# A spectral layer's results on four 64x64 TensorE tiles, and a last stage with small end chunks and zero-padded matmuls

## The chip, the cores and the metric

The kernel runs on one core of one Trainium2 chip. The metric is the time of one execution on the device, in microseconds (us). Before the change it is 1813.42 us, the median of three runs (1812.36 to 1813.81). The profiled execution took 1810.9 us; its trace spans 1809.2 us from the first to the last instruction, and every position in time below is counted from that span's start.

## What is computed

The input is an image batch of 4 x 56 x 56 positions with 128 channels, fp32. Layer 0 normalises in groups and adds a 7 x 7 neighbourhood attention. Layer 1 sees the image as 3136 tokens; it adds a linear attention, and then a spectral filter whose result is added to the same tokens:

```python
t = t + _L1_attn_ref(_ln_t(t), ...)
t = t + _L1_ffn_ref(_ln_t(t), ...)   # causal convolutions by FFT, 16 filters, then 128x128 matrices
```

Only the spectral filter's last part and the final sum are touched here. The convolution is done as small Fourier transforms, written as matmuls against constant tables. The image's rows and columns are transformed separately: 42 row frequencies (`N1 = 42`), and for each of them 28 column points (`NM = 28`), with real and imaginary parts, for two halves of the rows (`NS = 2`), two column parities `p`, four images and 128 channels.

## The kernel before

The program has three stages. `layers` (to about 780 us) does both attentions and the forward row transforms. `spectral_layer` (about 780 to 1658 us) goes over the 42 row frequencies. `onto_the_rest` (about 1659 us to the end) transforms back over the rows and adds the result to the tokens.

**The spectral loop** (L1570) is a software pipeline with one pass of the loop for one row frequency, 20.33 us each. TensorE's order is the program's own there (`manual_schedule` for PE); the other engines' orders are chosen when the program is built. A pass does, on TensorE: eight times `matrices` (L1487) alternating with seven times `product` (L1510); then `token_points` (L1466) for the next frequency; then `columns` (L1536) for the frequency three passes back. `columns` transforms results back over the columns: four matmuls, one for each row half `s` and column parity `p`, with 56 rows and 56 columns of the array in use and 512 moving columns. Operands of parity `p` lie in partitions 64p to 64p+55, and so do the results, so parity 0 uses the array's upper left quarter and parity 1 its lower right one. Each result has a PSUM bank of its own, and four copies (`evacuate`, L167 to L174, alternately on ScalarE and VectorE) bring them to `zs`. `store_columns` (L1554) writes `zs` to `zd` in DRAM.

PSUM has eight banks: three called `g0`, three `g1`, one `x`, one `py`. Each `g` name is handed out in turn, so a request gets the bank of the third request before it. `matrices` takes two `g0` and two `g1` at each call. `token_points` takes `x` and one `g0` and fills both; VectorE copies them to `us` (L1481), and ScalarE makes a negated copy of a part (L1482, `nc.scalar.mul`). `columns` takes two `g1` and two `g0`. So the first `g0` of the next pass's first `matrices` call is the bank that `token_points` had, and the second is that of the first parity-1 result of `columns`.

**The last stage** (L1600) loads 28 pairs of image columns in seven chunks of four (`WC = 4`). For each chunk and each half `q` of the width it loads tokens `tl` (ScalarE's DMA queue) and spectra `z` (SyncE's queue; 84 partitions, 1344 KB), does for each pair of columns four matmuls (84 rows, 56 columns, 512 moving columns; halves `q` in PSUM partitions 0 and 64), multiplies and adds on VectorE (L1634), and stores the chunk (L1639). The pool has three buffers for each name. It takes its memory after the spectral pools are given back, and as a whole.

Of the kernel before, what the change touches and what calls it, by code (L numbers as in the profile page):

```python
# [10 lines left out]
F32 = mybir.dt.float32  # L11
# [4 lines left out]
P = 128  # L16
B, H, W, C = 4, 56, 56, 128
# [39 lines left out]
NS, BR = 2, H // 2  # L57
N1, N2, NM = 42, W, W // 2
# [6 lines left out]
HALF = 2 * NM  # L65


def spectral_tables():

    m1 = np.arange(N1)  # L70
    m = m1[:, None] + N1 * np.arange(NM)[None]
    row = np.exp(-2j * np.pi * (m1[None] + 0.25) * np.arange(H)[:, None] / N1)
    rows = np.stack([row.real, row.imag], 1)
    into = np.zeros((P, 2 * N1))
    for g in range(NG):
        into[32 * g : 32 * g + BR] = rows[:BR].reshape(BR, -1)
    tok, back = np.zeros((2, N1, P, 2, NM))
    fil = np.zeros((N1, P, 2, NM, 2))
    for p in range(2):
        col = np.arange(p, N2, 2)  # L80

        fwd = np.exp(-2j * np.pi * (m[:, None, :] + 0.25) * col[None, :, None] / (2 * NP))

        bwd = np.exp(2j * np.pi * (m[:, :, None] + 0.25) * col[None, None, :] / (2 * NP)) / NP
        for part, turn in enumerate((1, 1j)):
            at = slice(64 * p + NM * part, 64 * p + NM * (part + 1))
            for to, a in ((tok, turn * fwd), (back, turn * bwd)):
                to[:, at] = np.stack([a.real, a.imag], 2)

            a = turn * fwd  # L90
            fil[:, 64 * part + NM * p : 64 * part + NM * (p + 1), p] = np.stack([a.real, a.imag], 3)

    onto = np.zeros((2, N1, NS, H))
    for s in range(NS):
        at = np.arange(H - BR * s)
        e = np.exp(2j * np.pi * (m1[:, None] + 0.25) * at[None] / N1)
        onto[0, :, s, BR * s :] = e.real
        onto[1, :, s, BR * s :] = -e.imag
    sign = np.ones((P, 1))
    sign[BR:N2] = sign[64 + BR : 64 + N2] = -1.0  # L100
    f = lambda a: np.ascontiguousarray(a, np.float32)
    return {
        "into": f(into),
        "taps_in": f(rows.reshape(H, -1)),
        "tok": f(tok.reshape(N1, P, -1).transpose(1, 0, 2)),
        "fil": f(fil.reshape(N1, P, -1).transpose(1, 0, 2)),
        "back": f(back.reshape(N1, P, -1).transpose(1, 0, 2)),
        "onto": f(onto.reshape(2 * N1, -1)),
        "sign": f(sign),
    }  # L110
# [13 lines left out]
def hybrid_kernel(  # L124
# [23 lines left out]
    nc = tc.nc  # L148
# [19 lines left out]
    def evacuate(dst, src):  # L168

        flip[0] ^= 1  # L170
        if flip[0]:
            nc.scalar.copy(dst, src)  # L172
        else:
            nc.vector.tensor_copy(dst, src)  # L174
# [1238 lines left out]
    def spectral_layer():  # L1413


        with ExitStack() as ph:
# [37 lines left out]
            def parts():  # L1454

                for p in range(2):
                    for part in range(2):
                        yield slice(64 * p + NM * part, 64 * p + NM * (part + 1)), p, part
# [77 lines left out]
            def columns(m1, yg, zs, pz):  # L1536

                back = tables_of(m1)[2]
                for s in range(NS):
                    for p in range(2):  # L1540
                        at = slice(64 * p, 64 * p + HALF)
                        nc.tensor.matmul(  # L1542
                            pz[s][p][at],
                            back[at],
                            yg[at, s * B : (s + 1) * B].rearrange("p k e -> p (k e)"),
                            start=True,
                            stop=True,
                        )
                for s in range(NS):
                    for p in range(2):  # L1550
                        at = slice(64 * p, 64 * p + HALF)
                        evacuate(zs[at, s], pz[s][p][at])

            def store_columns(m1, zs):  # L1554
                for at, p, part in parts():
                    nc.sync.dma_start(
                        zd[p::2, part * N1 + m1].rearrange("w s b e -> w (s b e)"),
                        zs[at].rearrange("w s f -> w (s f)"),
                    )

            def bank(tag):
                if tag == "x":
# [6 lines left out]
            with tc.manual_schedule(engines={mybir.EngineType.PE}):  # L1569
                for it in range(-1, N1 + LAG):  # L1570
                    ap, az, au = it - 1, it - LAG, it + 1
                    if 0 <= it < N1:
                        gts[it] = sp.tile([P, 2, 2 * NM, C // 2, 2], F32, name="gt")
                        if it + 2 < N1:
                            xms[it + 2] = load_tokens(it + 2)
                    if 0 <= ap < N1:
                        ys = sp.tile([P, NM // 4, C], F32, name="ys")
                    if 0 <= az < N1:
                        zs = sp.tile([P, NS, B * C], F32, name="zs")
                    for n in range(8):  # L1580
                        if 0 <= it < N1:
                            matrices(it, gts[it], n)
                        if 0 <= ap < N1 and n < 7:
                            if n % 4 == 0:
                                py = ps_y.tile([P, 4, C], F32, name="py")
                            product(py, gts[ap], us2[ap % 2], n)
                            if n == 3 or n == 6:
                                evacuate(ys[:, n - n % 4 : n + 1], py[:, : n % 4 + 1])
                    if au < N1:
                        token_points(au, xms.pop(au), us2[au % 2], [bank("x"), bank("g0")])  # L1590
                    if 0 <= az < N1:
                        pz = [[bank(f"g{1 - p}") for p in range(2)] for s in range(NS)]
                        columns(az, ygs.pop(az), zs, pz)
                    if 0 <= ap < N1:
                        ygs[ap] = regroup(ap, ys)
                    if 0 <= az < N1:
                        store_columns(az, zs)
                    gts.pop(ap, None)

    def onto_the_rest():  # L1600

        with ExitStack() as ph:
            fin = ph.enter_context(tc.tile_pool(name="fin", bufs=3))
            ps_o = ph.enter_context(tc.tile_pool(name="ps_o", bufs=4, space=bass.MemoryType.PSUM))
            onto = fin.tile([2 * N1, NS, H], F32, name="onto", bufs=1)
            nc.sync.dma_start(onto, table["onto"].rearrange("p (s h) -> p s h", s=NS))
            rows_in = td.rearrange("b (h w) c -> h b w c", w=W)
            rows_out = ot.rearrange("b (h w) c -> h b w c", w=W)
            WC = 4
            for w0 in range(0, W // 2, WC):  # L1610
                tl = fin.tile([P, B, WC, C], F32, name="tl")
                zin = []
                for q in range(2):
                    ws = slice(q * BR + w0, q * BR + w0 + WC)
                    nc.scalar.dma_start(tl[64 * q : 64 * q + H], rows_in[:, :, ws])
                    z = fin.tile([2 * N1, WC, NS, B * C], F32, tag=f"z{q}", name=f"z{q}")
                    nc.sync.dma_start(
                        z, zd[ws].rearrange("w p s b e -> p w s (b e)")
                    )
                    zin.append(z)  # L1620
                for i in range(WC):
                    po = ps_o.tile([P, B, C], F32, name="po2")
                    for s in range(NS):
                        for q in range(2):
                            nc.tensor.matmul(  # L1625
                                po[64 * q : 64 * q + H].rearrange("p b c -> p (b c)"),
                                onto[:, s],
                                zin[q][:, i, s],
                                start=(s == 0),
                                stop=(s == NS - 1),  # L1630
                            )
                    for q in range(2):
                        at = slice(64 * q, 64 * q + H)
                        nc.vector.scalar_tensor_tensor(  # L1634
                            tl[at, :, i], po[at], hmask[at], tl[at, :, i], ALU.mult, ALU.add
                        )
                for q in range(2):
                    ws = slice(q * BR + w0, q * BR + w0 + WC)
                    nc.scalar.dma_start(rows_out[:, :, ws], tl[64 * q : 64 * q + H])  # L1639

    unfit = keep.tile([1, 1], mybir.dt.int32, name="unfit")
    layers(False, unfit)
# [61 lines left out]
```

## Time and profile before

| Stretch | us | PE busy | clock granted to PE | DMA busy share |
|---|---|---|---|---|
| 0 to 100 | 100 | 68.08 | 0.81 | 0.55 |
| 100 to 700 | 600 | 542.73 | 0.93 | 0.45 |
| 700 to 800 | 100 | 75.22 | 0.67 | 0.53 |
| 800 to 1680 | 880 | 854.11 | 0.98 | 0.38 |
| 1680 to 1780 | 100 | 97.72 | 0.50 | 0.90 |
| 1780 to 1809.2 | 29.2 | 20.03 | 0.50 | 0.48 |

PE is the matmul engine, PEld its weight loads, DVE is VectorE, ACT is ScalarE, POOL is GpSimd, SP is SyncE. An fp32 matmul of the program shows as two records. [...]records overlap; so PE can look fully busy while it does less than it could. The granted clock is a share of TensorE's full speed. The DMA share is over the core's 16 DMA engines. A line of the trace that ends in "[0.98 <-ACT us L1482]" says that the engine was idle for 0.98 us and that the instruction of that name released it.

### The profile page before, as it was taken

How to read it: one execution, taken by the hardware profiler on the slowest of the kernel's cores; microseconds unless marked ns; L12 is line 12 of the kernel's file. 1: busy time of each engine (PE TensorE's matmuls, PEld its weight loads, DVE VectorE, ACT ScalarE, POOL GpSimd, SP SyncE). 2: the span in 40 equal slices, each digit the busy share in tenths (PEclk: the TensorE clock that was granted, in tenths of full speed). 3: DMA queues.
4: the chain of work that ended last, by engine and by line, in shares of the span. 5: the costliest groups of instructions: out<-in, count | busy, mean ns of one | idle time of the engine just before them, and what ended most of it. 6: DMA issues, size and time to landing. Idle time of an engine off the chain costs nothing. (4 is left out here: it accounts for less than half of the span.)

```text
span 1809.2 us, 71326 instructions
## 1 busy us (share of the span) xinstructions
PE 1657.9 (92%) x31481; PEld 1237.5 (68%) x31481; DVE 1070.5 (59%) x2142; ACT 756.3 (42%) x1529; POOL 390.3 (22%) x803
## 2 busy tenths in 40 slices
PE   4887898899999998779999999999999999995997
PEld 3665677567867766368888887888888887883221
DVE  4776786678868764135666666565666666562232
ACT  2333533366455444324444544454444544451000
POOL 4242254437446434000010001000000001000000
PEclk9788989899999997659999999999999999997555
DMA  6545446544343334632333333433434333325996
GB/s 166 116 88 106 86 94 147 121 119 124 88 136 91 92 98 112 198 92 65 99 106 105 96 87 100 113 99 88 102 104 107 89 91 97 103 72 150 239 226 182
DMA packets 285099, 207.69 MB, mean 115 GB/s; under 512 B 105868, under 2 KB 255532, under 8 KB 284652
## 3 DMA queue, kind: packets, MB, share of 16 engines
q1 hardware_dynamic: 275876, 189.50, 41.1%
q10 hardware_dynamic: 8904, 13.53, 2.7%
q8 instruction: 250, 4.10, 1.0%
q14 instruction: 69, 0.57, 0.1%
HBM read 115.31 MB, written 87.64 MB: 112 GB/s over the span
## 5 line engine op out<-in xcount | busy, mean ns | idle before, releaser
L1505 DVE COPY gt<-pg 128x448 f32<-128x448 f32 x672 | 388.4, 619 | 303.3 <-PE pg L1495 303.3
L1505 ACT COPY gt<-pg 128x448 f32<-128x448 f32 x672 | 326.0, 538 | 358.1 <-PE pg L1495 358.1
L1495 PE MATMUL pg<-v,mats 32*128 32x112 f32 x10752 | 402.2, 286 | 5.6 <-DVE gt L1505 2.0
L1495 PEld LDWEIGHTS pg<-v,mats 32*128 32x128 f32 x10752 | 341.8, 190 | 93.3 <-issue 51.7
L1514 PE MATMUL py<-gt,us 128*32 128x128 f32 x9408 | 339.2, 283 | 0.8 <-ACT ys L172 0.8
L1514 PEld LDWEIGHTS py<-gt,us 128*32 128x32 f32 x9408 | 266.9, 137 | 32.9 <-ACT ys L172 1.0
L1484 POOL COPY us<-us 128x448 f32<-128x448 f32 x42 | 23.4, 556 | 819.7 <-DVE us L1481 819.7
L1165 ACT ACTIVATE e<-scores 126x768 f32<-126x768 f32 (+1 forms) x140 | 107.3, 767 | 117.6 <-PE scores L1149 91.7
L1169 DVE TENSOR_TENSOR e<-e,relb 126x768 f32<-126x768 f32 (+1 forms) x140 | 137.9, 986 | 28.8 <-ACT e L1165 28.2
L1625 PE MATMUL po<-z,onto 84*56 84x512 f32 x224 | 124.8, 1067 | 20.8 <-DMA tl<-td 16.0
L1193 DVE RECIPROCAL recs<-results 128x96 f32<-128x96 f32 (+1 forms) x140 | 99.5, 711 | 49.4 <-PE results L1179 48.5
L1149 PE MATMUL scores<-qT,kp 32*126 32x96 f32 (+1 forms) x2240 | 105.0, 300 | 7.9 <-ACT e L1165 7.4
L1149 PEld LDWEIGHTS scores<-qT,kp 32*126 32x126 f32 (+1 forms) x2240 | 81.4, 196 | 43.9 <-ACT e L1165 17.9
L1625 PEld LDWEIGHTS po<-z,onto 84*56 84x56 f32 x224 | 31.8, 207 | 113.8 <-issue 98.1
L1634 DVE SCALAR_TENSOR_TENSOR tl<-po,hmask,tl 56x512 f32<-56x512 f32 x56 | 42.0, 750 | 104.4 <-PE po L1625 103.8
L1472 PE MATMUL px<-tok,xm 56*128 56x56 f32 x672 | 86.8, 281 | 18.1 <-DMA v<-vd 18.1
L1472 PEld LDWEIGHTS px<-tok,xm 56*128 56x128 f32 x672 | 81.3, 194 | 24.2 <-issue 19.9
L1179 PE MATMUL results<-e,v_sb 126*32 126x96 f32 (+1 forms) x2240 | 78.7, 261 | 11.7 <-DVE aT L1194 10.2
L1542 PE MATMUL xx<-yg,back 56*56 56x512 f32 x336 | 83.5, 611 | 4.0 <-DMA yg<-yd 4.0
L1472 PE MATMUL xx<-tok,xm 56*128 56x56 f32 x672 | 86.9, 281 | 0.0
L812 PE MATMUL bk<-mu,ut 128*112 128x128 f32 x672 | 81.8, 279 | 3.5 <-POOL ut L798 1.5
L812 PEld LDWEIGHTS bk<-mu,ut 128*112 128x112 f32 x672 | 77.0, 185 | 7.0 <-POOL ut L798 1.7
(177 smaller groups left out, 2106.1 us busy)
## 6 DMA issues: line engine op xcount, KB each, us to landing
xd<-xs SPq DMA_DIRECT2D x112, 168.0 KB
xm<-xd SPq DMA_DIRECT2D x168, 112.0 KB
yd<-ys SPq DMA_DIRECT2D x168, 112.0 KB
yg<-yd SPq DMA_DIRECT2D x168, 112.0 KB
zd<-zs SPq DMA_DIRECT2D x168, 112.0 KB
z<-zd SPq DMA_DIRECT2D x14, 1344.0 KB
v_sb<-vpad SPq DMA_DIRECT2D x224, 63.0 KB
acc<-in_x_dram SPq DMA_DIRECT2D x28, 224.0 KB
```

The costliest lines, as they stand in the source:

```text
L812: nc.tensor.matmul(pt[:CP, g * C : (g + 1) * C], ut[:, t0 : t0 + 2 * CP - 1 : 2], mu[:, i, :], start=(i == 0), stop=(i == NAR - 1),)
L1149: nc.tensor.matmul(sp[:, h, c * nq : (c + 1) * nq], keys_of(x0, y0 + c * KH, KH)[hs], qTs[b, ty][hs, QR * x0 : QR * x0 + nq], start=True, ...
L1165: nc.scalar.activation(e.rearrange("k (h q) -> k h q", h=NH), sp, AF.Exp)
L1169: nc.vector.tensor_tensor(e, e, relb[qc].rearrange("k h c q -> k (h c q)"), ALU.mult)
L1179: nc.tensor.matmul(po[hs, i, :nq], ones[:kn] if i else v_sb[:kn, c, hs], e[:, h, c], start=(c == 0), stop=(c == 1),)
L1193: nc.vector.reciprocal(rec, po[:, 1, :nq])
L1472: nc.tensor.matmul(pu[p][:, HALF * k : HALF * (k + 1)], xm[at, k // B, k % B, :], tok[at], start=True, stop=True,)
L1495: nc.tensor.matmul(pg[g // 2][g % 2][:, 4 * NM * i : 4 * NM * (i + 1)], mats[rows, 4 * n + i, :], v[rows], start=True, stop=True,)
L1505: copy(gt[:, h, :, e0 : e0 + 4, :], pg[q][h][:, : 16 * NM].rearrange("p (i m c) -> p m i c", i=4, c=2),)
L1514: nc.tensor.matmul(py[32 * j : 32 * (j + 1), n % 4, :], us.rearrange("p c k m -> p (c k) m")[:, NSB * FIRST[p, c] : NSB * (FIRST[p, c] + 4 ...
L1542: nc.tensor.matmul(pz[s][p][at], back[at], yg[at, s * B : (s + 1) * B].rearrange("p k e -> p (k e)"), start=True, stop=True,)
L1625: nc.tensor.matmul(po[64 * q : 64 * q + H].rearrange("p b c -> p (b c)"), onto[:, s], zin[q][:, i, s], start=(s == 0), stop=(s == NS - 1),)
```

## The change

It does four things.

- **Results' transforms on four tiles.** In `columns` the row half `s` now picks the partitions of the result (64s to 64s+63) and the parity the bank. The table `back` is padded from 56 to 64 columns. The four matmuls use the four quarters of the array; two banks are taken in place of four, and two copies of 128 partitions replace four of 56. `zs` has another layout, so `store_columns` writes runs of 2 KB in place of 4 KB.
- **Small chunks at the ends.** The last stage goes in chunks of 1, 1, 2, 4, 4, 4, 4, 4, 2, 1, 1, with four buffers.
- **Padding.** `onto` becomes 128 x 64 and `z` 128 partitions. The padding is set to zero once, with one memset of `onto` and eight of `z` (four on VectorE, four on GpSimd). The `z` buffers are made once, so that the zeros stay.
- **Waits by tile.** The pool `fin` now waits for each tile whose memory it takes over (`reuse_waits="tile"`), not for whole pools. `onto` is loaded on ScalarE's queue.

```diff
-    tok, back = np.zeros((2, N1, P, 2, NM))
+    tok = np.zeros((N1, P, HALF))
+    back = np.zeros((N1, P, 64))
...
                         nc.tensor.matmul(
-                            pz[s][p][at],
+                            pz[p][64 * s : 64 * (s + 1)],
                             back[at],
                             yg[at, s * B : (s + 1) * B].rearrange("p k e -> p (k e)"),
...
+                for p in range(2):
+                    evacuate(zs[:, p], pz[p])
+
+            def store_columns(m1, zs):
+                to = zd.rearrange("(c p) r s b e -> c p r s (b e)", p=2)
                 for s in range(NS):
-                    for p in range(2):
-                        at = slice(64 * p, 64 * p + HALF)
-                        evacuate(zs[at, s], pz[s][p][at])
...
+                    for part in range(2):
+                        at = 64 * s + NM * part
+                        nc.sync.dma_start(to[:, :, part * N1 + m1, s], zs[at : at + NM])
...
-                        pz = [[bank(f"g{1 - p}") for p in range(2)] for s in range(NS)]
+                        pz = [bank("g1"), bank("g0")]
...
-            fin = ph.enter_context(tc.tile_pool(name="fin", bufs=3))
+            fin = ph.enter_context(tc.tile_pool(name="fin", bufs=4, reuse_waits="tile"))
...
-            onto = fin.tile([2 * N1, NS, H], F32, name="onto", bufs=1)
-            nc.sync.dma_start(onto, table["onto"].rearrange("p (s h) -> p s h", s=NS))
+            onto = fin.tile([P, NS, 64], F32, name="onto", bufs=1)
+            nc.vector.memset(onto, 0.0)
+            nc.scalar.dma_start(
+                onto[: 2 * N1, :, :H], table["onto"].rearrange("p (s h) -> p s h", s=NS)
+            )
+            zs = [
+                [fin.tile([P, 4, NS, B * C], F32, name=f"z{q}{i}", bufs=1) for q in range(2)]
+                for i in range(4)
+            ]
+            for i in range(4):
+                for q, e in enumerate((nc.vector, nc.gpsimd)):
+                    e.memset(zs[i][q][64:], 0.0)
...
-            WC = 4
-            for w0 in range(0, W // 2, WC):
+            steps = (1, 1, 2, 4, 4, 4, 4, 4, 2, 1, 1)
+            for n, wc in enumerate(steps):
+                w0 = sum(steps[:n])
...
                             nc.tensor.matmul(
-                                po[64 * q : 64 * q + H].rearrange("p b c -> p (b c)"),
+                                po[64 * q : 64 * (q + 1)].rearrange("p b c -> p (b c)"),
                                 onto[:, s],
                                 zin[q][:, i, s],
```

## The prediction

> **What bounds the kernel now.** I read the stretches of the span first. The change touches two: the spectral loop (DMA share 0.38, PE almost without gaps), and the last stage, where PE also looks busy but so does the DMA. For the loop I took the timeline at the end of one pass, where `columns` stands:
>
> ```profile
> 1208.60 1.93 PE L1542 MATMUL xx<-yg,back 56*56 56x512 f32 x8
> 1208.77 0.62 DVE L1481 COPY us<-px 128x448 f32<-128x448 f32 x1 [0.85 <-PE xx L1472]
> 1209.31 0.61 DVE L1481 COPY us<-xx 128x448 f32<-128x448 f32 x1
> 1209.49 0.36 ACT L1482 ACTIVATE us<-px 128x224 f32<-128x224 f32 x1 [1.72 <-DVE us L1481]
> 1209.74 0.57 ACT L172 COPY zs<-xx 56x512 f32<-56x512 f32 x1
> 1209.96 1.34 DVE L174 COPY zs<-xx 56x512 f32<-56x512 f32 x2
> 1210.21 0.36 ACT L1482 ACTIVATE us<-xx 128x224 f32<-128x224 f32 x1
> 1210.56 0.58 ACT L172 COPY zs<-xx 56x512 f32<-56x512 f32 x1
> ...
> 1210.62 0.30 PEld L1495 LDWEIGHTS pg<-v,mats 32*128 32x128 f32 x6 [0.98 <-ACT us L1482]
> ```
>
> `columns` is 2.02 us of PE (1208.60 to 1210.62), but the next pass's first weight load is not released by its end: it is released by ScalarE's second negated copy, which ends at 1210.57. The answer for that line says how often:
>
> ```profile
> L1482 ACT ACTIVATE us<-xx x42: 357/357/361, 784.1 to 1616.9; 128x224 f32<-128x224 f32 x42
> ...
>   PEld pg L1495: 37.4, 38
> ```
>
> 38 times is every pass that has a `columns` and a `matrices` after it. So `columns` lies beside a chain of VectorE copy, VectorE copy, ScalarE copy that empties the bank of `token_points`, and this chain ends last, by about 0.1 us.
>
> For the last stage I read its stretches (after the five engines' busy times come the granted clock, the DMA share and GB/s), then the DMA view of 1680 to 1780, then the end of the timeline:
>
> ```profile
> 1720.00:1740.00 20.00, 20.00 (x42) 5.35 (x41) 7.50 (x10) 0.00 (x0) 0.00 (x0) 0.50 0.90 221
> ...
> 1792.00:1794.00 2.00, 2.00 (x6) 0.54 (x5) 0.30 (x1) 0.00 (x0) 0.00 (x0) 0.50 0.01 3
> ...
> 1798.00:1800.00 2.00, 2.00 (x4) 0.43 (x2) 1.10 (x2) 0.00 (x0) 0.00 (x0) 0.50 0.00 0
> ```
>
> ```profile
> DMA packets 8071, 23.47 MB, mean 235 GB/s; under 512 B 393, under 2 KB 393, under 8 KB 8069
> ```
>
> ```profile
> 1801.01 1.53 DVE L1634 SCALAR_TENSOR_TENSOR tl<-po,hmask,tl 56x512 f32<-56x512 f32 x2 [1.90 <-PE po L1625]
> 1801.79 1.12 ACTq L1639 DMA_DIRECT2D out_dram<-tl  x2
> ```
>
> From 1660 to 1791 the DMA share is about 0.9 (0.82 to 0.94), at a mean of 235 GB/s; from 1792 to 1802 it is nothing, while the last chunk of four is computed (VectorE's adds come every 3.41 us), and only then do its two stores go out. The PE clock is 0.50 throughout. **The DMA bounds this stage, and its tail is bare.** What the stage moves, from the issue list: z 14 x 1344 KB, tl and output 14 x 448 KB each, 32.1 MB; at 235 GB/s that is 136.7 us of the 150.1 between the first z issue (1659.14) and the end (1809.2).
>
> **What the Trainium skill says.** (1) TensorEngine Tiling (Array Packing), section "Available Configurations": 64x64 gives four independent tiles. The trace has no such case; it has two 56*56 quarters side by side (pairs of records 0.43 us apart), and four 32-row tiles (32 records of `matrices` in 1.16 us). (2) TensorE: Matmul & The Clock Gate, Part 1: the clock is half or full, by how busy PE has lately been. The trace agrees on two values, but at 0.50 PE's records cover 20.00 of 20.00 us, so covering time is not what is counted; whether the used part of the array is, no row here decides. (3) DMA: Bandwidth & Descriptors, section "Why a DMA increments its semaphore by 16 and not by 1": a transfer uses the largest number of engines up to 16 that divides its slowest dimension, 14 for 84, 56 and 28 partitions. 14 of 16 is 0.875, and the stage sits at 0.90. So it is full, and the change keeps these partition counts.
>
> **Part 1, `columns` on four tiles, loop.** Removed: the four matmuls go in four slots of 0.43 us; with four tiles at once they need two, 0.86 us less, so PE would be free at about 1209.7. But the bank rotation decides. With one `g0` and one `g1` for `columns`, the next `matrices` call's first `g0` is the bank of its own last call, long empty, and its second `g0` is that of `token_points`. So PE starts two records and then waits for the same ScalarE copy. That copy's earliest time: VectorE's second copy ends 1209.92, the hop to ScalarE is 0.09 (1209.40 to 1209.49 for the first), the copy takes 0.36, the hop to PE 0.05: 1210.43, against 1210.62. That needs ScalarE to do it ahead of its copy of `zs`; before, the first `zs` copy went ahead (1209.74) and the second after. Now each `zs` copy needs results of both row halves, and the second half's copy stood after it. So I take the early order: 0.19 us. A second thing goes: `matrices`' third weight load (1210.71 in the trace) waited for VectorE's `zs` copy; that call took 1.17 us against 1.09 otherwise, 0.08. Sum 0.27 x 38 passes = **10 us**; with the old ScalarE order 0.08 x 38 = 3 us. The other 0.6 us that four tiles save lies beside the chain. Two copies of 0.69 and 0.58 that vanish cost nothing before either: both engines are idle between calls (1.0 to 1.2 us waits for pg).
>
> **Part 2, from the last frequency to the first z load.** The last `columns` waits for its load (1650.69), runs at half clock, 4.73 us; its last copy ends at 1656.15, the store follows and lands at about 1658.8. Two slots of 0.85 and the second round of copies go, some 2.5 us. Against it: a z load must wait for its buffer's memset. No row shows one on VectorE over more than five elements; the skill's VectorE: DVE Perf Modes, section "Zero memsets can be issued as uint32 (trn2)", says one cycle per element; with 0.96 GHz of its cycle table 4096 elements make an estimated 4.3 us. GpSimd's row (128x4464, 3.82 us) makes 3.5 us. The waits are by tile, so most memsets can go while the engines idle (1632 on, once `gt` is free); GpSimd is idle. Bounds: nothing, when VectorE's four fall in its gaps; 4.3 us, when one stands ahead of the last `zs` copy or the first buffer (over `back`, read to the end) is cleared last. I take 1.5, net **1 us** gained. Behind a late VectorE copy queue `store_columns` on SyncE, then z. The 2 KB runs of the store cost nothing: in the trace's packet records 2048 B took 84 to 116 ns and 4096 B 178 to 260.
>
> **Part 3, chunks.** Bytes unchanged. Runs of tl shrink to 512 B in single-column chunks; packet records give 29.5 ns for 512 B (100 to 600 us) against 116 for 2048 B, the same per byte, so 0. At the end: four columns' stores are left when the last z lands, 0.92 MB; so loads finish 0.9 + (32.1 - 0.92)/0.235 = 133.6 us after the first z issue. Then one half's four records 3.4 us, pipe 0.25, adds 1.5, and store to end, before 6.65 us with 0.92 MB, now 0.23 MB: about 3.95. Sum 142.7. Up to 0.46 MB of tl can come ahead by the waits by tile, 2 us. 140.7 against 150.1: **9 us** gained. More issues (66 for 42, about 0.3 to 0.5 us each on two queues) hide behind transfers.
>
> **Part 4, padding.** Cost: nothing[...]. Gain: only if the clock doubles, and then in the bare tail alone, 1.7 us, as the DMA bounds the rest. I count none.
>
> Sum: 10 + 1 + 9 = 20 us, 1793.
>
> **The rivals.** *ScalarE keeps its old order* (zs between the two negated copies): the saved matmul slots turn into waiting; 3 + 1 + 9 = 13, 1800. For it: two tiles' time in the first copy's readiness is not longer than before if all four run at once. *All goes well*: full clock, memsets hidden, stores early: 1788. *The tail's gain is spent* on memsets ahead of the zs copies and on loads held by buffer waits: 1806. Against it: 0.9 share held in spite of many such waits before. *Slower*: VectorE takes a `zs` copy between the two `us` copies; the gate then moves by 0.7 + 0.1 us in 38 passes, +30, less 10: about 1833. Against it: both `us` copies are ready together, ahead of any result of `columns`.
>
> **How the numbers follow.** Main case 1793: 0.50. Old order 1800: 0.30. All well 1788: 0.08. Tail spent 1806: 0.06. Slower 1833: 0.06. The range leaves out the slow case and most of the spent tail at the top and the luckiest at the bottom: 1788 to 1804. Faster 0.92, same 0.02, slower 0.06.
>
> **What would show it.** In the profile after: `columns` records in two slots, about 1.1 us; PEld of pg still waiting for ACT us L1482, some 30 us in all (with the old order 37); a pass of 20.06 us (old order 20.25); in the last stage DMA share still 0.90, and the bare stretch under 5 us. The prediction is wrong if that wait vanishes (then up to 35 us come from the loop), if 64x64 tiles don't overlap, if the DMA share falls below 0.85 between the first and the last load, or if memset rows stand ahead of the last zs copies.

## The result, and the profile after

The changed kernel takes 1791.1 us, the median of four runs (1789.66 to 1791.56). The kernel before, run beside it, takes 1812.89 us (four runs, 1807.94 to 1813.81). The ratio is 0.9884, 95% interval 0.9865 to 0.9903. The forecast was 1793 in 1788 to 1804. The sum came out; of its four parts only the first did.

I cut both traces at the same instructions. "First z issue" is the first load of spectra in the last stage.

| us | before | after | difference | forecast |
|---|---|---|---|---|
| start to the first `token_points` (not touched) | 779.1 | 781.1 | +2.0 | 0 |
| from there to the start of the last `columns` | 871.6 | 863.1 | -8.5 | -10 |
| to the first z issue | 8.45 | 8.99 | +0.5 | -1 |
| to the end | 150.0 | 136.0 | -14.0 | -9 |
| span | 1809.2 | 1789.2 | -20.0 | -20 |

The first stretch is the same code in every kernel below, and in their traces it lasts 772.0 to 781.4 us. So whole times scatter by several us of their own, and effects of a few us are read here from the stretches, not from medians.

**The loop.** This is the timeline of the changed kernel at the end of one pass: start, duration, engine, line, operation, and in brackets how long the engine was idle and what released it.

```profile
1185.78 1.09 PE L1543 MATMUL xx<-yg,back 56*64 56x512 f32 x8
1185.95 0.63 DVE L1482 COPY us<-px 128x448 f32<-128x448 f32 x1 [0.85 <-PE xx L1473]
1186.49 0.61 DVE L1482 COPY us<-xx 128x448 f32<-128x448 f32 x1
...
1186.80 0.48 PE L1496 MATMUL pg<-v,mats 32*128 32x112 f32 x4
1187.03 0.69 DVE L175 COPY zs<-xx 128x512 f32<-128x512 f32 x1
...
1187.20 0.36 ACT L1483 ACTIVATE us<-xx 128x224 f32<-128x224 f32 x1 [0.17 <-DVE us L1482]
1187.46 0.58 ACT L173 COPY zs<-xx 128x512 f32<-128x512 f32 x1
1187.61 0.65 PEld L1496 LDWEIGHTS pg<-v,mats 32*128 32x128 f32 x20 [0.51 <-ACT us L1483]
1187.61 0.71 PE L1496 MATMUL pg<-v,mats 32*128 32x112 f32 x16 [0.33 <-ACT us L1483]
```

Eight records of `columns` now take 1.09 us where they took 1.93: 64x64 quarters do run four at a time, as the Trainium skill lists them (TensorEngine Tiling (Array Packing), "Available Configurations"). But PE does only four records of `matrices` (1186.80) and then stops for ScalarE's second negated copy (1187.20 to 1187.56), which now goes ahead of ScalarE's `zs` copy. From the start of `columns` to the end of that gate it was 1.97 us and is 1.78. The answer for the line of the negated copy, who waited for it:

```profile
L1483 ACT ACTIVATE us<-xx x42: 351/357/362, 786.1 to 1609.6; 128x224 f32<-128x224 f32 x42
...
  PEld pg L1496: 19.4, 38
  PE pg L1496: 12.7, 38
```

The wait is still there in 38 passes: 19.4 us of idle time of the weight loads, where it was 37.4 us before, and 12.7 us of the matmuls. The two lie beside each other and don't add up.

**The link and the last stage.** By the link I mean the time from the last `columns` to the first z issue. The first line below is that of the store's issue instructions in the changed kernel (shortest, median, longest ns; first and last start), followed by that of before. Then come the changed kernel's timeline around the last `columns` and at the end, and its stretches (busy us of PE, PEld, VectorE, ScalarE, GpSimd with the numbers of instructions, granted clock, DMA share, GB/s).

```profile
L1558 SPq DMA_DIRECT2D zd<-zs x168: 789/835/1852, 866.2 to 1650.6; - x168
```

The same line of the kernel before:

```profile
L1556 SPq DMA_DIRECT2D zd<-zs x168: 306/384/1798, 865.2 to 1656.5; - x168
```

The timeline and the stretches of the changed kernel:

```profile
1644.23 2.97 PE L1543 MATMUL xx<-yg,back 56*64 56x512 f32 x8 [6.89 <-DMA yg<-yd]
...
1647.32 0.69 DVE L175 COPY zs<-xx 128x512 f32<-128x512 f32 x1 [9.15 <-PE xx L1543]
...
1648.08 3.30 SPq L1558 DMA_DIRECT2D zd<-zs  x4
...
1649.06 3.47 DVE L1616 MEMSET z<- 64x4096 f32 x1 [0.91 <-issue]
...
1779.61 1.93 PE L1638 MATMUL po<-z,onto 128*64 128x512 f32 x6 [1.01 <-DMA z<-zd]
1779.95 4.43 ACTq L1652 DMA_DIRECT2D out_dram<-tl  x6
1781.58 1.53 DVE L1647 SCALAR_TENSOR_TENSOR tl<-po,hmask,tl 56x512 f32<-56x512 f32 x2 [3.40 <-PE po L1638]
```

```profile
1700.00:1720.00 20.00, 8.96 (x22) 2.69 (x21) 2.83 (x4) 0.00 (x0) 0.00 (x0) 0.66 0.92 234
1720.00:1740.00 20.00, 16.96 (x54) 5.09 (x49) 10.49 (x14) 0.00 (x0) 0.00 (x0) 0.91 0.91 291
...
1770.00:1774.00 4.00, 3.65 (x14) 1.27 (x14) 1.71 (x3) 0.00 (x0) 0.00 (x0) 1.00 0.66 227
...
1780.00:1782.00 2.00, 1.54 (x6) 0.27 (x2) 0.42 (x1) 0.00 (x0) 0.00 (x0) 1.00 0.91 330
1782.00:1784.00 2.00, 0.00 (x0) 0.00 (x0) 1.08 (x2) 0.00 (x0) 0.00 (x0) 1.00 0.82 248
1784.00:1786.00 2.00, 0.00 (x0) 0.00 (x0) 0.00 (x0) 0.00 (x0) 0.00 (x0) 0.58 0.56 143
1786.00:1789.20 3.20, 0.00 (x0) 0.00 (x0) 0.00 (x0) 0.00 (x0) 0.00 (x0) 0.50 0.03 10
```

Four things are to be seen. A store of results has an issue instruction of 835 ns (median); before it was 384. After the last copy to `zs` SyncE spends 3.30 us on four of them (1648.08 to 1651.38), then waits some 1.6 us for them to land, as before, and issues the first z load at 1653.22. The ten bare us of before are gone: from 1778 to 1784 the DMA share is 0.82 or more. But it isn't full up to there: from 1760 to 1778, where the chunks get small, it is 0.66 to 0.80. And the granted clock in the last stage, 0.50 throughout before, is now between 0.50 and 1.00 (mean 0.76 while z is loaded), and PE is no longer covered from end to end.

### The profile page after: what moved, and what is told of

It reads as the page before. It is cut to its first block, busy times and chain, and to the rows that moved or that the text cites. A ratio compares the mean times of both kernels' runs of the same rounds, so it can differ in the third digit from the quotient of the medians.

```text
span 1789.2 us, 71383 instructions
## 1 busy us (share of the span) xinstructions
PE 1594.2 (89%) x31481; PEld 1236.1 (69%) x31481; DVE 1053.1 (59%) x2105; ACT 738.0 (41%) x1487; POOL 406.1 (23%) x807
## 4 chain that ended last, share of the span: by engine, by line
PE 66%; DMA 14%; DVE 6%; POOL 6%; SPq 4%; issue 2%; ACT 2%; ACTq 0%; DVEq 0%; POOLq 0%
PE pg L1496 21%; PE py L1515 18%; PE px L1473 4%; PE results L1180 4%; PE scores L1150 3%; DMA tl<-td 3%; SPq L220 3%; PE bk L813 2%; PE bk L878 2%; PE xx L1543 2%; DMA m_raw<-in_M_minus_dram 2%; DMA out_dram<-tl 2%; POOL v L520 2%; DMA z<-zd 2%; PE bk L718 1%
## 5 line engine op out<-in xcount | busy, mean ns | idle before, releaser
L1496 PE MATMUL pg<-v,mats 32*128 32x112 f32 x10752 | 416.3, 286 | 14.7 <-ACT us L1483 12.7
L1496 PEld LDWEIGHTS pg<-v,mats 32*128 32x128 f32 x10752 | 349.2, 190 | 106.5 <-issue 48.5
L1638 PE MATMUL po<-z,onto 128*64 128x512 f32 x224 | 78.4, 743 | 56.0 <-DMA z<-zd 54.6
L1638 PEld LDWEIGHTS po<-z,onto 128*64 128x64 f32 x224 | 25.9, 164 | 109.3 <-issue 71.3
L1180 PE MATMUL results<-e,v_sb 126*32 126x96 f32 (+1 forms) x2240 | 78.6, 260 | 10.7 <-DVE aT L1195 9.1
L1473 PEld LDWEIGHTS xx<-tok,xm 56*128 56x128 f32 x672 | 81.3, 194 | 0.0
```

Of the source, the lines that this page charges most:

```text
L1180: nc.tensor.matmul(po[hs, i, :nq], ones[:kn] if i else v_sb[:kn, c, hs], e[:, h, c], start=(c == 0), stop=(c == 1),)
L1473: nc.tensor.matmul(pu[p][:, HALF * k : HALF * (k + 1)], xm[at, k // B, k % B, :], tok[at], start=True, stop=True,)
L1496: nc.tensor.matmul(pg[g // 2][g % 2][:, 4 * NM * i : 4 * NM * (i + 1)], mats[rows, 4 * n + i, :], v[rows], start=True, stop=True,)
L1638: nc.tensor.matmul(po[64 * q : 64 * (q + 1)].rearrange("p b c -> p (b c)"), onto[:, s], zin[q][:, i, s], start=(s == 0), stop=(s == NS - 1),)
```

## The theories, and the experiments

My theory was that of the forecast: the loop's gain is set by the negated copy's bank, and the last stage's gain comes from the small end chunks, with the padding worth nothing. The rivals are that the four tiles' slots are what counts in the loop, and that the padding, not the chunks, carries the last stage. All ratios are against the kernel before on the same chip.

### Each half of the change alone

The first kernel has only the loop's part; its last stage is the old one. The second has only the last stage's part:

```diff
# first: the last stage as before
-            fin = ph.enter_context(tc.tile_pool(name="fin", bufs=4, reuse_waits="tile"))
+            fin = ph.enter_context(tc.tile_pool(name="fin", bufs=3))
...
-            steps = (1, 1, 2, 4, 4, 4, 4, 4, 2, 1, 1)
+            WC = 4
# second: columns, evacuate and store_columns as before
-                            pz[p][64 * s : 64 * (s + 1)],
+                            pz[s][p][at],
...
-                        pz = [bank("g1"), bank("g0")]
+                        pz = [[bank(f"g{1 - p}") for p in range(2)] for s in range(NS)]
```

> Only the loop's part of the change (columns on four tiles, two banks, two copies, the 2 KB stores); the last stage is the old one. Theory (a pass is gated by ScalarE's second negated copy, so of 0.86 us saved on PE only some 0.2 us a pass counts, and the stores' longer issues cost 1.7 us after the last pass): a pass of 20.12 us, first z issue some 8 us earlier against the start of the loop, last stage still 150 us, time about 1805. Rival (the loop gains the 0.86 us a pass that four tiles save, and the last stage gives it back): first z issue 30 us earlier.

> Only the last stage's part (end chunks, padding, waits by tile); columns is the old one. Theory (the stage is bound by its transfers and gains at its bare tail, by tl loads ahead, and a little by rate, whatever the loop does): first z issue to the end 136 us against 150, time about 1799, and with the loop's part alone the two savings add up to that of both, 22 us. Rival (the stage's gain hangs on the loop's part, through buffers or the order of queues): 1803 or more.

The loop's part alone: 1799.89 us, ratio 0.9929 (0.991 to 0.9949). Its pass is 20.05 us (before 20.33, after 20.11). Counted from the first `token_points`, the first z issue comes 9.0 us earlier than before; 8 us were expected, and 30 by the rival. From the start of the last `columns` to the end it takes 160.1 us where before takes 158.5: the loop's part *loses* 1.6 us outside the loop. The last stage's part alone: 1793.39 us, ratio 0.9895 (0.9876 to 0.9914); the loop is as before (871.6 us), and from the last `columns` to the end it takes 139.8 us. Both times are some 5 us below the expected ones. The expectation that the two savings add up was wrong.

So both halves gain, but they don't add: 0.71% and 1.05% make 1.76%, and the whole change gives 1.16%. The traces show 5.2 us of the difference after the loop, where the whole change takes 145.0 us and the second half alone 139.8. Of these, 2.1 us are the link (8.99 against 6.89). There the new stores cost twice. Their issues take 2.2 us longer. And with the old stores SyncE waited only 0.3 us for landings, with the new ones 1.6. By the program, an old store held one column parity, so the first chunk, one column wide, needed two of the last four stores only; a new store holds both parities, so it needs all four. That is read from the traces and the program, and not tested by itself. Against this, slots and copies save 1.8 us of the link. The other 3 us are a slower stage (136.0 against 132.9); the loads come at 240 and 249 GB/s. Why is open, and with single traces it may be scatter: two traces of the same kernel differ by 0.8 us there, and a kernel with the loop's part in the last experiment has 133.9.

### The last stage taken apart

Three kernels differ from the changed one by one thing in the last stage: no padding and no memsets; equal chunks of four; waits by pool.

```diff
# no padding
-            onto = fin.tile([P, NS, 64], F32, name="onto", bufs=1)
-            nc.vector.memset(onto, 0.0)
+            onto = fin.tile([2 * N1, NS, H], F32, name="onto", bufs=1)
...
-                    e.memset(zs[i][q][64:], 0.0)
...
-                                po[64 * q : 64 * (q + 1)].rearrange("p b c -> p (b c)"),
+                                po[64 * q : 64 * q + H].rearrange("p b c -> p (b c)"),
# equal chunks
-            steps = (1, 1, 2, 4, 4, 4, 4, 4, 2, 1, 1)
+            steps = (4, 4, 4, 4, 4, 4, 4)
# waits by pool
-            fin = ph.enter_context(tc.tile_pool(name="fin", bufs=4, reuse_waits="tile"))
+            fin = ph.enter_context(tc.tile_pool(name="fin", bufs=4))
```

> The changed kernel without padding: 84 rows and 56 columns again, no memsets, buffers of 84 partitions; chunks and waits by tile stay. Theory (DMA bounds the stage; the clock counts only after the last load): clock back at 0.50 in the last stage, loads end at about the same time as with padding, the tail 2 to 3 us longer, time 1793 to 1794. Rival 1 (padding and the full clock gave the 5 us that the stage gained beyond the forecast, by freeing buffers earlier): 1796 to 1799. Rival 2 (the memsets held the first loads back): 1789 or less.

> The changed kernel with seven chunks of four columns, padding and waits by tile kept. Theory (the small chunks at the end fill the bare tail): bare stretch without transfers back, of four columns at whatever clock holds (1.7 us each at full, 3.4 at half), time 1796 to 1801. Rival (the tail is short once the clock is full, and the gain came from tl loads ahead and a better rate): 1791 to 1793.

> The changed kernel with the pool waiting for whole pools again (all else as changed). Theory (the memsets and the first tl loads run beside the end of the loop only thanks to the waits by tile): all eight memsets after the last store, the first z load behind a memset of 3.5 to 4.3 us, and the first tl loads not ahead: 4 to 7 us longer, 1795 to 1798. Rival (neither was on the path): 1791.

Their times are 1790.71, 1795.25 and 1791.11 us, ratios 0.9874 (0.9851 to 0.9897), 0.9903 (0.9881 to 0.9925) and 0.9906 (0.9875 to 0.9938). The intervals overlap with that of the changed kernel, so the times alone tell none apart. By its time the first fits none of its three theories, the second lies just under its theory's range, and the third fits the rival by which waits by tile are worth nothing. The stretches say more:

| us | last `columns` to first z issue | first z issue to end | both |
|---|---|---|---|
| before | 8.45 | 150.0 | 158.5 |
| after, two traces | 8.99, 9.07 | 136.0, 136.8 | 145.0, 145.8 |
| no padding | 9.17 | 147.4 | 156.6 |
| equal chunks | 11.91 | 139.3 | 151.2 |
| waits by pool | 12.97 | 137.1 | 150.0 |

Small chunks are worth 5.8 us beside the mean of the two traces (151.2 less 145.4), half of it in the stage (139.3 less 136.4) and half in the link. In the link SyncE waits 4.4 us for the last stores to land, in place of 1.6, while token loads of 448 KB, not 112, are under way beside them. In the stage the bare tail is back with equal chunks, although the clock is high there:

```profile
1780.00:1784.00 4.00, 4.00 (x14) 1.33 (x12) 1.79 (x3) 0.00 (x0) 0.00 (x0) 0.79 0.03 10
1784.00:1788.00 4.00, 3.10 (x10) 0.81 (x8) 3.53 (x6) 0.00 (x0) 0.00 (x0) 1.00 0.02 4
```

Waits by tile are worth 4.6 us (150.0 less 145.4), of which 3.9 are in the link: by pool, all eight memsets stand behind the last stores, and the first z waits for its memset. With waits by tile GpSimd's four memsets go beside the loop's last frequencies. The groups of the changed kernel from 1620 us on give the price (instructions, then busy us in sum and mean ns of one):

```profile
L1616 DVE MEMSET z<- 64x4096 f32 x4 | 13.9, 3472 | 3.3 <-issue 2.5 <-DVE z L1616 0.8
L1616 POOL MEMSET z<- 64x4096 f32 x4 | 14.0, 3516 | 17.8 <-PE py L1515 14.8 <-issue 3.1
```

On VectorE they start 4.27 us apart, which is what the prediction estimated (4.3) from one cycle an element, as the Trainium skill has it (VectorE: DVE Perf Modes, "Zero memsets can be issued as uint32 (trn2)"); the record is shorter, 3.47 us.

The surprise is the padding: without it the stage is 11 us longer, and 147.4 us is nearly the old 150.0 in spite of small chunks, four buffers and waits by tile. The expectation had the loads end at about the same time and only the tail 2 to 3 us longer. In the trace the loads end 8.6 us later. But the times didn't show it: the profiled execution, 1795.68 us, was the slowest of five, and their median of 1790.71 gives the lowest ratio of the three. So the run was repeated.

### Is it the padding, and is it the clock?

Four kernels on one chip: the changed kernel again; again without padding; padding alone on the kernel before (its chunks of four, three persistent z buffers, waits by pool); and the changed kernel with `onto` padded to 64 columns but only 84 rows.

```diff
# padding alone: chunks, waits and loop of before, and
-            onto = fin.tile([2 * N1, NS, H], F32, name="onto", bufs=1)
+            onto = fin.tile([P, NS, 64], F32, name="onto", bufs=1)
+            nc.vector.memset(onto, 0.0)
...
+                    e.memset(zs[i][q][64:], 0.0)
...
-                                po[64 * q : 64 * q + H].rearrange("p b c -> p (b c)"),
+                                po[64 * q : 64 * (q + 1)].rearrange("p b c -> p (b c)"),
# 84 rows, 64 columns: the changed kernel, and
-            onto = fin.tile([P, NS, 64], F32, name="onto", bufs=1)
+            onto = fin.tile([2 * N1, NS, 64], F32, name="onto", bufs=1)
...
-                    e.memset(zs[i][q][64:], 0.0)
```

> The changed kernel once more, beside the three others of this call on one chip, so that small differences can be read. Expected: 1789 to 1793, last stage 134 to 138 us, loads ending 122 to 128 us after the first z issue, clock changing between 0.5 and 1 with a mean of 0.75 or more.

> The kernel without padding once more. In its first profile the last stage took 147 us, though its times lay by those of the changed kernel. Theory A (padding shortens the loads: at the higher clock a z buffer comes free earlier and the DMA share never falls): last stage 142 us or more again, shares under 0.8 in some stretch before the last load, median 4 to 10 us above the changed kernel on this chip. Theory B (that profile was an outlier, and padding is worth the tail's 2 to 3 us): last stage 137 to 140, median 1 to 3 us above.

> The kernel before with the padding alone (buffers made once, three of them; chunks of four, waits by pool). Theory A (the clock rises and the transfers get faster with it): mean rate up to the last load 240 GB/s or more against 233, loads 122 to 124 us, bare tail shorter by 7 us at full clock, memsets ahead of the first z load cost 4: together 8 to 12 us faster than before. Theory B (the clock is worth its bare tail alone): rate 233, 3 us faster.

> The changed kernel with the columns padded to 64 and the rows left at 84: no memsets of z. Used part of the array 84 x 128 of 128 x 128, 0.66, against 0.57 without and 1 with both. If the granted clock goes by the used part with a bound below 0.66, or by columns: clock as in the changed kernel, and its time or a little less. If by rows, or with a bound above 0.66: clock 0.50 as without padding, and that kernel's time.

| | us | ratio, interval | both stretches | stage | loads end after the first z issue | from there to the end | clock while z loads |
|---|---|---|---|---|---|---|---|
| after again | 1788.69 | 0.9887 (0.9868 to 0.9906) | 145.8 | 136.8 | 126.1 | 10.7 | 0.76 |
| no padding | 1794.99 | 0.9928 (0.9908 to 0.9948) | 156.2 | 147.0 | 133.7 | 13.2 | 0.50 |
| 84 rows, 64 columns | 1795.01 | 0.9915 (0.99 to 0.9929) | 156.1 | 146.7 | 133.5 | 13.1 | 0.50 |
| padding alone | 1804.45 | 0.9977 (0.9965 to 0.9989) | 150.5 | 138.8 | 121.6 | 17.2 | 0.80 |

On one chip the padding is worth 6.3 us of the median, with intervals that don't overlap, and 10.3 us of the two stretches. The stage agrees in all four traces with and without it (136.0 and 136.8; 147.4 and 147.0). Padded columns without padded rows do nothing: the clock stays at 0.50 and the stage at 146.7. So it is neither the four buffers nor the padded columns by themselves. It goes with the clock, and the clock rises when the matmuls use 128 rows and 64 columns of each half. Whether the rows decide, or the used share of the array (0.66 with 84 rows, 1 with both, and the bound somewhere between), no run here tells apart.

Padding alone takes 11 us off the old stage too (138.8 against 150.0) and gives 3.3 back in memsets ahead of the first z (11.74 against 8.45). By these stretches it gains 8.0 us, the low end of theory A. By the medians it gains 4.5 us, between the theories; its profiled execution, 1799.42 us, was the second fastest of 21. The rate, on which theory A counted, hardly rose: 236 GB/s up to the last load (at most 240 with the packets that this trace lacks) against 234 before. What the higher clock gave here is a shorter end (17.2 us against 22.6 after the loads) and loads that end 5.8 us sooner with more of the stores still to come.

Why the clock of an engine matters in a stage with a full DMA can be read from the stretches of the second kernel without padding:

```profile
1724.00:1734.00 10.00, 10.00 (x22) 2.96 (x20) 4.50 (x6) 0.00 (x0) 0.00 (x0) 0.50 0.90 195
1734.00:1744.00 10.00, 8.30 (x16) 1.77 (x14) 1.64 (x3) 0.00 (x0) 0.00 (x0) 0.50 0.66 202
1744.00:1754.00 10.00, 10.00 (x21) 2.71 (x20) 4.36 (x6) 0.00 (x0) 0.00 (x0) 0.50 0.90 223
1754.00:1764.00 10.00, 10.00 (x21) 2.81 (x19) 3.09 (x5) 0.00 (x0) 0.00 (x0) 0.50 0.74 230
```

The DMA share falls to 0.66 and 0.74 in the middle of the stage, while PE is covered for 8.30 to 10.00 of 10 us. How close PE is to its own limit at half clock, a line of the kernel before shows: 32 records, as many as a chunk of four has, span 18.4 us,

```profile
1767.76 18.36 PE L1625 MATMUL po<-z,onto 84*56 84x512 f32 x32 [0.18 <-DMA z<-zd]
```

and the transfers of a chunk take an estimated 19.6 us (4.59 MB, a seventh of the stage's 32.1, at 234 GB/s). The margin is some 1 us a chunk. When PE falls behind, its results are stored later, and later loads wait for that: in the queue of SyncE z loads waited 61.6 us in sum for the landing of stores (35.4 in the changed kernel), and 0.3 us for PE directly. The changed kernel has a share of 0.91 to 0.95 from 1656 to 1760; it too falls to 0.66 to 0.80 from 1760 to 1778, where its chunks get small. That the dips are PE's doing is read from the overlap, not tested by itself; that padded rows and columns take 8 us off the time of the loads is measured.

A high share is not a full rate, either. The changed kernel's stretches 1700 to 1720 and 1720 to 1740, shown above, have shares of 0.92 and 0.91 with 234 and 291 GB/s. Up to the last load the rate is 240 GB/s with padding and 227 without, at shares of 0.89 and 0.87.

The 84-row kernel shows where the clock does not rise:

```profile
1720.00:1740.00 20.00, 20.00 (x39) 5.87 (x36) 6.66 (x10) 0.00 (x0) 0.00 (x0) 0.50 0.91 214
1740.00:1760.00 20.00, 18.66 (x34) 5.04 (x32) 7.06 (x10) 0.00 (x0) 0.00 (x0) 0.50 0.78 210
```

PE is covered for 20.00 of 20 us, at 0.50. In the padded kernel it is covered for 16.96 and granted 0.91. The Trainium skill says that the clock goes by how busy PE has been (TensorE: Matmul & The Clock Gate, Part 1); these runs say that busy there can't mean covered time, and that padding with zeros counts as use. 128 rows without the padded columns were not run.

### The gate in the loop

If PE waits in each pass for a bank that ScalarE's negated copy still reads, then the gain lies in taking that copy off the bank. It can read VectorE's copy in SBUF in place of the bank. One kernel is the changed one with this edit, the other the kernel before with it:

```diff
-                    nc.scalar.mul(us[:, 6 + 2 * p], src[:, 1], -1.0)
+                    nc.scalar.mul(us[:, 6 + 2 * p], us[:, 2 * p + 1], -1.0)
```

> The changed kernel with one more edit: the negated copies read us in SBUF, written just before by VectorE, not the PSUM banks, so a bank is free after VectorE's copy. Theory (ScalarE's second negated copy is the gate, and the rest of four tiles' saving is hidden behind it): the wait of the next pass's weight loads for ScalarE goes, the gate is VectorE's second copy 0.45 us earlier, a pass of 19.65 to 19.75 us, 1773 to 1777. Rival (another wait stands right behind it: VectorE's zs copy, the py bank or the first gt copies): a pass of 20.0 or more, 1787 or more.

> The kernel before with the same edit alone (negated copies read us in SBUF). Theory (in the kernel before, the columns matmuls end only 0.1 us ahead of the gate, so freeing the gate uncovers them): a pass 0.0 to 0.2 us shorter than 20.33, time 1806 to 1813; so the gain of the same edit is three or more times larger with four tiles. Rival (the gate costs both kernels the same): 17 us shorter here too, 1796.

On the changed kernel: 1771.32 us, ratio 0.9785 (0.9761 to 0.981). The pass falls from 20.11 to 19.70 us, and the loop's stretch from 863.1 to 846.9. On the kernel before: 1811.15 us, ratio 1.0002 (0.9987 to 1.0016), pass 20.36. The same edit is worth 16 us on one and nothing on the other. First the timeline of the changed kernel with it, then that of the kernel before with it, each at the end of a pass:

```profile
1175.49 1.09 PE L1543 MATMUL xx<-yg,back 56*64 56x512 f32 x8
...
1176.23 0.61 DVE L1482 COPY us<-xx 128x448 f32<-128x448 f32 x1
...
1176.41 0.86 ACT L1483 ACTIVATE us<-us 128x224 f32<-128x224 f32 x2 [1.75 <-DVE us L1482]
1176.51 1.36 PEld L1496 LDWEIGHTS pg<-v,mats 32*128 32x128 f32 x32 [0.81 <-DVE us L1482]
1176.51 1.53 PE L1496 MATMUL pg<-v,mats 32*128 32x112 f32 x32
```

```profile
1208.62 1.93 PE L1542 MATMUL xx<-yg,back 56*56 56x512 f32 x8
...
1209.53 0.39 ACT L1482 ACTIVATE us<-us 128x224 f32<-128x224 f32 x1 [1.75 <-DVE us L1481]
...
1210.00 1.31 DVE L174 COPY zs<-xx 56x512 f32<-56x512 f32 x2
...
1210.47 1.25 PEld L1495 LDWEIGHTS pg<-v,mats 32*128 32x128 f32 x32 [0.82 <-DVE us L1481]
1210.47 1.42 PE L1495 MATMUL pg<-v,mats 32*128 32x112 f32 x32
```

In the first, `matrices` begins 1.02 us after the start of `columns`, as in the changed kernel, and after four records waits for VectorE's second copy (to 1176.85) in place of ScalarE's. It goes on 1.41 us after the start of `columns`; the changed kernel goes on after 1.83. In the second it begins after 1.85 us, when the slots of `columns` are over, does four records, and then waits for VectorE's first copy of a result to `zs`, which ends at 1210.70 and frees the next bank. It goes on 2.13 us after the start of `columns`, and the kernel before after 2.11. So in the kernel before two more gates stand right behind the negated copy: the four slots of `columns`, and the copy of its first parity-1 result. The change takes both away, with four tiles and with two banks in place of four; which of the two counts more, no run tells. Only the change and the free bank together pay. This settles the theory against its rival: slots saved on PE alone are not what the changed kernel gained. The copy from SBUF costs 390 ns against 357, off the path.

### The stores' issue time

On top of that kernel, for the last two row frequencies half of the results' stores go on ScalarE's queue:

```diff
-                        nc.sync.dma_start(to[:, :, part * N1 + m1, s], zs[at : at + NM])
+                        (nc.scalar if part and m1 >= N1 - 2 else nc.sync).dma_start(
+                            to[:, :, part * N1 + m1, s], zs[at : at + NM]
+                        )
```

> The changed kernel with the negated copies read from SBUF and, for the last two row frequencies alone, half of the zd stores issued on ScalarE's queue. Theory (after the last copies the first z load waits for four store issues of 0.84 us one after the other): two issues' time less, first z issue 1.5 us nearer to the last columns than in the kernel with the negated copies alone; time 1 to 2 us less than it. Rival (the stores' landing, not their issue, sets it): no difference.

1770.13 us, ratio 0.9786 (0.9759 to 0.9813): by the time it can't be told from the kernel it builds on. From the last copy to `zs` to the end of the last issue it takes 1.83 us in place of 3.37, so 1.5 us are saved there, as expected. But the link goes only from 9.27 to 8.57 us: 0.4 us are lost to a longer landing (2.27 us from the last issue to the first z load, against 1.84), and 0.4 us ahead of the last copy. The whole after the last `columns` goes from 145.3 to 142.4; most of that is in the stage, which this edit doesn't touch, and is not explained by it. The issues cost about the same on either queue:

```profile
L1558 SPq DMA_DIRECT2D zd<-zs x164: 789/837/1785, 859.8 to 1627.6; - x164
L1558 ACTq DMA_DIRECT2D zd<-zs x4: 805/868/1746, 1617.4 to 1627.6; - x4
```

So a store of these has an issue of 0.84 to 0.87 us wherever it goes, and two at a time are sooner done. These two last kernels are the fastest here, and beat both the kernel before and the changed one.

## Why the prediction was right, point by point

**What bounds the loop, and Part 1: right.** The gate is the negated copy; ScalarE took it in the early order; the wait stayed; the records take two slots (1.09 us, 1.1 forecast). Of the two terms, the gate's 0.19 us is measured as 0.19 (1.97 to 1.78). The 0.08 is 0.09 (gate to the first `product`: 1.17 to 1.08). The pass is 0.22 us shorter, not 0.27: the second and third `product` of a pass take 1.10 us each to the next `matrices`, and took 1.07, for a reason I don't know. The loop's part alone has a pass of 20.05 us (20.06 forecast). In eight traces with this loop the stretch is 8.5 to 10.2 us shorter, for 10 forecast. One sign was missed: the weight loads' wait is 19.4 us, and some 30 were forecast, since four loads now go ahead of it. The warning that up to 35 us would come from the loop if that wait vanished points the right way: when it did, 16 more came.

**Part 2: wrong in sign.** The failing step is "The 2 KB runs of the store cost nothing". It looked only at what the packets take on the DMA engines. What changed is the issue: 56 runs of 2 KB in place of 28 of 4 KB take SyncE 0.84 us in place of 0.38. From the end of the last `zs` copy to the start of the last store's issue it was 0.38 us before and is 2.58. The 2.5 us that slots and copies were to save were too many: from the start of the last `columns` to the end of the last copy it was 5.46 us and is 3.78, so 1.7 less. The second round of copies had lain beside the matmuls. The memset term was sized at 1.5 us and came to nothing; in the changed kernel VectorE's first memset of z (1649.06 to 1652.53) ends before the stores have landed, and the first z goes at 1653.2. Sum: 1.7 saved and 2.2 lost, so 0.5 us lost, where 1 gained was forecast.

**Part 3: the tail did shrink, but the size came by luck.** The bare stretch shrank to the last 3.2 us with 10 GB/s and 2 us before them at 143. But Part 3 reckoned at half clock, and the kernels that run so, those without padded rows, have a stage of 146.7 to 147.4 us: chunks, buffers and waits by tile together gain some 3 us there, and 9 were forecast. Their loads end 133.5 to 134.0 us after the first z issue, where the forecast had them (133.6); the term that failed is the rest, 9.1 us less up to 2 for tokens loaded ahead, which is 13.1 to 13.4. With padding it is 10.6, and the loads end at 125.4. More than the assumed 0.92 MB was left to store: from 1778 to 1786 the DMA moved some 2 MB (304, 330, 248 and 143 GB/s in 2 us each). One of the forecast's own signs of being wrong was seen, too: the DMA share falls below 0.85 between the first and the last load (0.80 from 1760 to 1770, 0.66 from 1770 to 1774).

**Part 4: wrong.** The step is "as the DMA bounds the rest. I count none." A DMA share of 0.90 and PE records over 20.00 of 20 us stood in the same line, and I took the first for the bound and the second for show. Both were near their limit, and a share of 0.9 left room for a higher rate. The padded matmuls got the high clock in most of the stage, and are worth 10 to 11 us of it. That they cost nothing on PE was right: at full clock their loads of weights, and so their slots, are 0.43 us apart (1780.09, 1780.52).

So the total was near by luck. Padding, put at nothing, gave the 11 us that made good chunks and waits (some 3 of 9 us), and a loop and a link that each came to 1.5 us less than forecast; and the untouched first stretch of that trace was 2.0 us longer. Without the padding the stage would have been 147 us and not the 140.7 of the sum.

**What stays open.** It is open why the last stage is 3 us slower with the loop's part than without it (136.0 and 132.9), if it is more than scatter. It is also open why a 4096 B packet of a z load takes 257 to 262 ns in the mean in every kernel without padded rows and in the one with padding alone, and 229 to 248 in those with four buffers and padding. And the clock's rule is open: rows, or used share.

## What to carry to other kernels

When two limits stand close to full in the same stretch, count the second as a bound too: a cheap edit that lifts it (here zeros around the operands) can pay even though the first looks saturated. When a wait is set by who still reads a buffer, shorten the reading; freeing PE slots beside it gave 0.2 us a pass, and both together 0.6. A transfer's new layout has a price on the issuing queue as well as on the DMA engines, and it shows where the queue's next instruction is on the path.

## What the runs showed of the hardware

- In the last stage the granted clock stayed at 0.50 with 84 rows, with 56 and with 64 columns of each half in use, and PE covered for 20.00 of 20 us. With 128 rows, 44 of them zeros, and 64 columns of each half, its mean while z was loaded was 0.75 to 0.80, and it was 1.00 at times.
- An issue of a store with 56 runs of 2 KB took 0.84 us on SyncE and 0.87 on ScalarE's queue; with 28 runs of 4 KB it took 0.38 on SyncE.
- At full clock, four 64x64 tiles took eight fp32 records of 512 columns in 1.09 us; two 56x56 quarters took 1.93.
- The DMA moved 234 GB/s at a busy share of 0.92 and 291 GB/s at 0.91 in two neighbouring stretches of one trace.
- VectorE's memset of 64x4096 has a record of 3.47 us, but the next one starts 4.27 us after it.
